# Three weight turns: two by VectorE blocks and transfers, one behind attention

## The chip, the cores and the metric

The kernel runs on one core of one Trainium2 chip. The metric is the device time of one execution in microseconds; lower is better. It is given as the median over several runs. One further execution was profiled, and the engine times below are from it.

## The reference

One image of 256 channels and 48 x 48 positions, that is 2304 tokens, goes through two layers, all in float32.

- Layer 0: group norm, then q, k and v projections (`xt @ Wq.T` and so on, so the weights are needed turned), an attention in which every head of every token is a row of one softmax over 9216 keys of width 64, the output projection `O @ Wo.T + bo`, and the residual.
- Layer 1, attention part: layer norm, `h = x @ W0 + b0`, slice weights `sw = softmax(h @ Ws + bs)`, an attention between 64 slice tokens, and `out @ Wout + bout`, with the residual.
- Layer 1, experts: layer norm, gate logits `xf @ Wg + bg`, the best two of 8 experts per token, a GELU network of width 1024 in each, and the residual.

The kernel folds small products of weights: `W0 @ Ws` gives the slice logits straight from the tokens, and `Wout @ Wg` (with `bout @ Wg`) gives the part of the gate logits that comes out of layer 1's attention. To multiply such a product on TensorE, W0 and Wout must stand turned in SBUF, as `W0T` and `WoutT`.

## The kernel before, in words

**Projections (0 to 66 us).** SyncE issues all loads in written order: x, Wq, Wk, Wv, Wo, some biases, W0, Ws, Wqkv, Wg, Wout in eight pieces, and two stores of zeros. `transposed` turns a 256 x 256 matrix by four TensorE transposes of 128 x 128 into one PSUM bank (`pw`), which ScalarE copies to SBUF. Wq, Wk and Wv are turned ahead of the projections, Wo after the first block of tokens, W0 and Wout after the first of the 18 tiles of v. `slice_weights` multiplies W0T and Ws into `Wl`, `centred` takes the mean out of `Wl`, and `gate_weights` multiplies WoutT and Wg into the last eight columns of `Wout_sb` and `bout_bc`. These stand in the loop over the v tiles, at `i == 3`, `6` and `9`. Nothing here is issued in a fixed order except what goes through `pe`, `dve`, `act` or `pool`: a scheduler places the plain `nc.` instructions. PSUM's eight banks are five for `pp` (q, k and v), one for `pgb` and two for `pw`.

**Attention of layer 0 (66 to 1216 us).** 18 blocks (`b`) of 512 query rows each run over 36 pairs of key tiles. `scores` makes two banks of `s` on TensorE, ScalarE takes the exponential into `p`, `times_values` multiplies it by v into two banks of `av`, and VectorE adds up `p` in `acc`. All of these engines' instructions stand in written order. Small steps of the finished blocks (`follow`, `between`) are strewn in between; their results use the banks `pa` and `pb` of pool `ps_side`. `out_proj` needs WoT, first for block pair g = 0. Its `move` brings VectorE's 32 x 32 blocks of `turned` to their places by 32 transfers per two token tiles, issued by SyncE (line 466). PSUM's banks are taken in the order of the pools: `ps_s` (0 to 3), `ps_av` (4, 5), `ps_side` (6, 7).

**Behind attention (1216 to 1260 us).** The last block is closed apart: `between(NQB - 1, ...)` sums `both` over the partitions into `pb` on TensorE and adds `busy(4, pa)`, four matmuls of 256 columns whose results nobody reads; `invert_few` turns `pb` on VectorE, inverts it and turns it back into `rinv`; `divide` makes `OT`. `out_proj` of the last group follows (`pm`), then `slices`, the turned slice weights (`pt`, `swT`), `busy(2, spin)`, and the sums `pts` and `den` once `sw` is there. Later `Wout_sb` with its gate columns is used once, for `tw`.

The last two steps in the block's closing, as written:

```python
half = close(behind, last=True)
invert_few, divide, extremes = between(NQB - 1, behind)
invert_few()
half(1, pool)
half(0, dve)
divide()
```

**Routing and experts (1260 us to the end).** Top-2 choice, slots, gathered rows, two matmul layers per slot, and the output.

## Time and profile before

| | us |
|---|---|
| Median of three runs | 1588.09 (1587.11 to 1591.71) |
| The profiled execution, its own time | 1585.05 |
| its span | 1583.3 |
| TensorE busy in it | 1561.7 |
| VectorE busy | 1037.0 |
| ScalarE busy | 829.6 |
| GpSimd busy | 257.6 |
| First scores of attention start at | 66.47 |
| Last matmul into `av` starts at | 1214.5 |

The names of a row are out<-in by the program's tiles, with buffer numbers left out. L61 is the line of the helper through which `pe`, `dve`, `act` and `pool` issue, so the tiles tell those rows apart. PE is TensorE, DVE VectorE, ACT ScalarE, POOL GpSimd, and SPq the queue on which SyncE issues transfers. A float32 matmul is recorded as two passes, so one turn of a matrix by four transposes is x4 and a product of two 256-column pieces is x4 as well. In a timeline a row is: start, time, engine, line, operation, tiles, shape, count, and in brackets the idle time just before it and what ended that.

### The profile page before, as it was taken

The page shows a single profiled execution, that of the slowest core. Times are in us where ns is not written, and L with a number is a line of the kernel's source. Part 1 is how long each engine was busy: PE and PEld are TensorE (multiplying, and loading weights), DVE is VectorE, ACT ScalarE, POOL GpSimd, SP SyncE. Part 2 cuts the span into 40 slices and gives each one's busy share as a digit, 9 for nine tenths or more (in the row PEclk, how much of TensorE's full clock was granted, in tenths as well). Part 3 has the DMA queues.
Part 4 walks back from the last instruction along what each step waited for, and adds up shares of the span by engine and source line. Part 5 has one row for each costly group of instructions (what it writes and reads, how often), then busy time and mean ns, then how long its engine had stood idle before and what let it go on. Part 6 is the DMA issues. An engine that isn't in the chain of part 4 may idle for free. (4 is left out here: it accounts for less than half of the span.)

```text
span 1583.3 us, 32283 instructions
## 1 busy us (share of the span) xinstructions
PE 1561.7 (99%) x13123; PEld 780.2 (49%) x13123; DVE 1037.0 (65%) x1324; ACT 829.6 (52%) x1168; POOL 257.6 (16%) x198
## 2 busy tenths in 40 slices
PE   9999999999999999999999999999999999999998
PEld 5633343333333333333333333333334789999996
DVE  7578787787777778878778778787787631211112
ACT  3356565565665656556556566566564533333331
POOL 0001001011010010110101101101010135766661
PEclk9999999999999999999999999999999999999999
DMA  4000000000000000000000000000000956666665
GB/s 137 1 1 1 1 1 3 6 1 1 9 1 1 8 1 2 7 2 2 4 5 2 2 8 1 1 8 1 1 2 21 335 168 177 186 180 190 194 172 160
DMA packets 52750, 79.32 MB, mean 50 GB/s; under 512 B 22527, under 2 KB 43214, under 8 KB 47470
## 3 DMA queue, kind: packets, MB, share of 16 engines
q1 hardware_dynamic: 42834, 66.45, 13.0%
q0 software_dynamic: 9104, 10.10, 3.8%
q8 instruction: 108, 1.77, 0.5%
q10 hardware_dynamic: 652, 0.56, 0.1%
q14 instruction: 52, 0.43, 0.1%
HBM read 62.94 MB, written 12.32 MB: 48 GB/s over the span
## 5 line engine op out<-in xcount | busy, mean ns | idle before, releaser
L61 ACT ACTIVATE p<-s 128x1024 f32<-128x1024 f32 x648 | 662.7, 1023 | 471.1 <-PE s L61 469.3
L61 DVE TENSOR_TENSOR acc<-acc,p 128x1024 f32<-128x1024 f32 x612 | 749.1, 1224 | 243.5 <-ACT p L61 237.6
L61 PE MATMUL av<-p,v_sb 64*64 64x512 f32 x5184 | 675.7, 590 | 3.2 <-ACT p L61 2.0
L61 PE MATMUL s<-q,kk 64*64 64x512 f32 x5184 | 674.8, 589 | 0.5 <-DVE tn L61 0.5
L61 PEld LDWEIGHTS s<-q,kk 64*64 64x64 f32 x5184 | 202.1, 133 | 353.6 <-issue 181.5
L61 PEld LDWEIGHTS av<-p,v_sb 64*64 64x64 f32 x5184 | 195.6, 131 | 358.7 <-ACT p L61 201.7
L61 POOL PARTITION_ALL_REDUCE total<-both x17 | 71.1, 4185 | 1011.8 <-ACT p L61 833.8
L61 ACT ACTIVATE hid<-ph,bcol 128x128 f32<-128x128 f32 x312 | 88.7, 369 | 197.6 <-PE ph L61 145.5
L61 PEld LDWEIGHTS ph<-xT,w 128*128 128x128 f32 x1248 | 145.2, 192 | 3.9 <-issue 1.7
L61 PE MATMUL ph<-xT,w 128*128 128x128 f32 x1248 | 145.9, 275 | 1.2 <-PEq L1398 0.7
L61 PE MATMUL py<-w_sb,hid 128*128 x624 | 144.0, 379 | 0.9 <-issue 0.7
L61 DVE TENSOR_TENSOR y<-py,b_bc 128x256 f32<-128x256 f32 x39 | 16.5, 424 | 176.1 <-PE py L61 136.9
L61 PEld LDWEIGHTS py<-w_sb,hid 128*128 128x128 f32 x624 | 114.6, 190 | 15.2 <-issue 1.3
L1244 POOL DMA_INDIRECT xs<-tn_d,part_t x88 | 90.0, 1022 | 29.9 <-issue 25.9
L1244 POOL DMA_INDIRECT t_d<-y,slot_t x38 | 61.3, 1613 | 77.4 <-DVE xT L61 32.7
L61 DVE COPY xT<-pt 128x256 f32<-128x256 f32 x17 | 7.0, 424 | 57.0 <-PE pt L61 57.0
L61 DVE RECIPROCAL rinv<-rinv 128x256 f32<-128x256 f32 x17 | 29.7, 1745 | 0.0
L61 POOL TENSOR_TENSOR rstd_t<-ve,mhalf 128x2 f32<-128x2 f32 (+2 forms) x13 | 11.1, 850 | 104.9 <-DVE ve L61 97.3
L61 DVE TENSOR_TENSOR acc<-p 128x1024 f32<-128x1024 f32 x18 | 22.1, 1225 | 4.9 <-ACT p L61 3.3
L340 DVE TENSOR_SCALAR q<-pp,bcol 64x512 f32<-64x512 f32 (+1 forms) x30 | 20.8, 694 | 5.9 <-PE pp L323 5.4
L61 DVE TENSOR_REDUCE up<-av 128x512 f32<-128x1024 f32 x17 | 20.8, 1224 | 5.0 <-PE av L61 5.0
L61 PE MATMUL spin<-Wqkv_sb,ident 128*128 128x256 f32 x82 | 19.2, 382 | 0.0
(306 smaller groups left out, 618.5 us busy)
## 6 DMA issues: line engine op xcount, KB each, us to landing
w<-in_L_ffn_W_dram SPq DMA_DIRECT2D x39, 1024.0 KB
w_sb<-in_L_ffn_W_dram SPq DMA_DIRECT2D x8, 1024.0 KB
t_sb<-turned SPq DMA_DIRECT2D x224, 8.0 KB
x_sb<-in_x_dram SPq DMA_DIRECT2D x3, 576.0 KB
t_d<-t_sb SPq DMA_DIRECT2D x2, 768.0 KB
tn_d<-tn SPq DMA_DIRECT2D x2, 768.0 KB
t_sb<-t_d SPq DMA_DIRECT2D x3, 512.0 KB
out_dram<-ob SPq DMA_DIRECT2D x3, 512.0 KB
```

What stands on the lines that cost most here:

```text
L61: return self.tc.keep_in_program_order(getattr(self.engine, name)(*args, **kwargs))
L340: nc.vector.tensor_scalar(dst, pq[rows, 0:tn], bcol[rows, B_Q + m : B_Q + m + 1], 0.125, ALU.add, ALU.mult,)
L1244: new = nc.gpsimd.indirect_dma_start(**kwargs)
```

## The change

- `turned_by_blocks` is new. VectorE turns the 32 x 32 blocks of a 256 x 256 matrix in one instruction of 128 x 512, and 32 transfers on SyncE's queue, each 32 rows of two runs of 128 bytes, bring the blocks to their places. Wo and W0 go this way, both called after the first block of tokens.
- `slice_weights` and `centred` stand at `i == 9` and `13` of the v loop instead of `3` and `6`.
- `gate_weights` is gone. Wout is turned by TensorE into `pa` after the last block of attention, where `busy(4, pa)` becomes four transposes and `busy(3, pb)`; ScalarE copies it into `turned`. The product with Wg takes the place of `busy(2, spin)`, in bank `spin`, and ScalarE copies it out.
- Attention's PSUM pools are opened in the order `ps_av`, `ps_side`, `ps_s`.
- `brep` has two parts instead of four.

```diff
+        def turned_by_blocks(dst, raw, name):
+
+            t = pj.tile([P, 2, C], FP, name=f"{name}_turned")
+            nc.vector.transpose(t.rearrange("p c n -> p (c n)"), raw.rearrange("p c n -> p (c n)"))
+            for a in range(4):
+                for k in range(4):
+                    for co in range(2):
+                        nc.sync.dma_start(
+                            out=dst[k * 32 : (k + 1) * 32, :, co * P + a * 32 : co * P + (a + 1) * 32],
+                            in_=t[a * 32 : (a + 1) * 32, co, :].rearrange("r (ci k s) -> r ci k s", ci=2, k=4)[
+                                :, :, k, :
+                            ],
+                        )
+            return dst
...
             if bi == 0:
                 later_constants()
-                transposed(WoT, raws["Wo"])
+                turned_by_blocks(WoT, raws["Wo"], "Wo")
+                W0T = turned_by_blocks(pj.tile([P, 2, C], FP, name="W0T"), W0_sb, "W0")
...
-            for k, b in enumerate((B_0, B_0 + 1, B_OUT, B_OUT + 1)):
+            for k, b in enumerate((B_0, B_0 + 1)):
...
-        def gate_weights():
...
-        brep = pj.tile([P, 4, P], FP, name="brep")
+        brep = pj.tile([P, 2, P], FP, name="brep")
...
-            if i == 0:
-                W0T = transposed(pj.tile([P, 2, C], FP, name="W0T"), W0_sb)
-                WoutT = transposed(pj.tile([P, 2, C], FP, name="WoutT"), Wout_sb)
-            elif i == 3:
+            if i == 9:
                 slice_weights()
-            elif i == 6:
+            elif i == 13:
                 centred()
-            elif i == 9:
-                gate_weights()
...
-        ) as at_p, tc.tile_pool(name="att1", bufs=1) as at_1, tc.tile_pool(name="ps_s", bufs=2, space=PSUM) as ps_s, tc.tile_pool(
+        ) as at_p, tc.tile_pool(name="att1", bufs=1) as at_1, tc.tile_pool(
             name="ps_av", bufs=1, space=PSUM
-        ) as ps_av, tc.tile_pool(name="ps_side", bufs=1, space=PSUM) as ps_side:
+        ) as ps_av, tc.tile_pool(name="ps_side", bufs=1, space=PSUM) as ps_side, tc.tile_pool(
+            name="ps_s", bufs=2, space=PSUM
+        ) as ps_s:
...
-                    busy(4, pa)
+                    for ci in range(2):
+                        for co in range(2):
+                            pe.transpose(
+                                pa[:, (2 * ci + co) * P : (2 * ci + co + 1) * P],
+                                Wout_sb[:, co, ci * P : (ci + 1) * P], ident,
+                            )
+                    busy(3, pb)
...
+                def keep_turned():
+                    act.copy(turned.rearrange("p c n -> p (c n)"), pa)
+
...
             invert_few()
+            keep_turned()
...
-    busy(2, spin)
+    gates = spin[:, 0 : 3 * E].rearrange("p (c e) -> p c e", c=3)
+    for ci in range(2):
+        for k in range(2):
+            pe.matmul(
+                gates[:, ci, :], turned[:, k, ci * P : (ci + 1) * P], Wl[:, k, S : S + E],
+                start=(k == 0), stop=(k == 1),
+            )
+    for k in range(2):
+        pe.matmul(
+            gates[:, 2, :], bcol[:, B_OUT + k : B_OUT + k + 1].to_broadcast([P, P]), Wl[:, k, S : S + E],
+            start=(k == 0), stop=(k == 1),
+        )
+    act.copy(Wout_sb[:, :, C : C + E], gates[:, 0:2, :])
+    act.copy(bout_bc[:, C : C + E], gates[:, 2, :])
```

More of the change, by code (lines that the diff above doesn't have):

```diff
@@ L379, in centred @@
             )
-        def gate_weights():
-            pw = ps_w.tile([P, 512], FP, name="pw", tag="pw")
-            for ci in range(2):
-                for k in range(2):
-                    nc.tensor.matmul(
-                        pw[:, ci * E : (ci + 1) * E], WoutT[:, k, ci * P : (ci + 1) * P],
-                        Wl[:, k, S : S + E], start=(k == 0), stop=(k == 1),
-                    )
-            for k in range(2):
-                nc.tensor.matmul(
-                    pw[:, 2 * E : 3 * E], brep[:, 2 + k, :], Wl[:, k, S : S + E],
-                    start=(k == 0), stop=(k == 1),
-                )
-            nc.vector.tensor_copy(
-                Wout_sb[:, :, C : C + E], pw[:, 0 : 2 * E].rearrange("p (c e) -> p c e", c=2)
-            )
-            nc.vector.tensor_copy(bout_bc[:, C : C + E], pw[:, 2 * E : 3 * E])
-        brep = pj.tile([P, 4, P], FP, name="brep")
+        brep = pj.tile([P, 2, P], FP, name="brep")
         for i in range(NTT):
@@ L734, in extremes @@
                     dve.tensor_reduce(ends_of[:, 1, b : b + 1], rinv, AX.X, ALU.max)
+                def keep_turned():
+                    act.copy(turned.rearrange("p c n -> p (c n)"), pa)
                 if b == NQB - 1:
-                    return invert_few, divide, extremes
+                    return invert_few, divide, extremes, keep_turned
                 work.extend([(12, sides), (13, invert), (14, divide), (15, extremes)])
@@ L772, in attention @@
             half = close(behind, last=True)
-            invert_few, divide, extremes = between(NQB - 1, behind)
+            invert_few, divide, extremes, keep_turned = between(NQB - 1, behind)
             invert_few()
+            keep_turned()
             half(1, pool)
```

## The prediction

> **What bounds the kernel now.** I read the page's busy table first, then its clock slices, then the timelines of the two stretches that the change touches.

> ```profile
> PE 1561.7 (99%) x13123; PEld 780.2 (49%) x13123; DVE 1037.0 (65%) x1324; ACT 829.6 (52%) x1168; POOL 257.6 (16%) x198
> ```

> TensorE is busy for 99% of the span, so a microsecond taken out of its stream, or put into it as a wait, is a microsecond of the end. The change touches only the projections (0 to 66 us) and the stretch behind attention (1215 to 1242 us). TensorE's timeline of the first:

> ```profile
> 47.11 0.60 PE L61 MATMUL pw<-ident,W_sb 128*128 128x128 f32 x4
> 47.55 0.60 PE L61 MATMUL pw<-ident,Wout_sb 128*128 128x128 f32 x4
> 47.98 2.75 PE L404 MATMUL pp<-WvT,t_sb 128*128 128x256 f32 x12
> 50.58 1.00 PE L358 MATMUL pw<-Ws_sb,W0T 128*128 128x64 f32 x8
> ...
> 57.54 0.95 PE L386 MATMUL pw<-Wl,WoutT 128*128 128x8 f32 x8
> 58.35 0.59 PE L391 MATMUL pw<-Wl,brep 128*128 128x8 f32 x4
> 58.80 7.15 PE L404 MATMUL pp<-WvT,t_sb 128*128 128x256 f32 x32
> 66.47 1.95 PE L61 MATMUL s<-q,kk 64*64 64x512 f32 x16 [0.52 <-DVE tn L61]
> ```

> There is no gap until 66.47, where the first scores wait 0.52 us for VectorE's last v eviction. To cost transfers that SyncE issues, its timeline: its last load, the first two lines of the existing transfers of this very shape (32x2x32, 64 runs of 128 bytes), and their row by source line.

> ```profile
> 21.53 0.70 SPq L224 DMA_DIRECT2D t_d<-empty  x1
> ...
> 269.66 11.91 SPq L466 DMA_DIRECT2D t_sb<-turned  x17
> ```
> ```profile
> 280.98 10.49 SPq L466 DMA_DIRECT2D t_sb<-turned  x16
> ```
> ```profile
> L466 SPq DMA_DIRECT2D t_sb<-turned x224: 585/595/1692, 269.7 to 1056.8; - x112
> ```

> One issue occupies SyncE for 595 ns. A burst of 32 takes 21.8 us (269.66 to 291.46), 0.68 us each. The seven bursts lie between 21.2 and 22.5 us.

> The stretch behind attention, TensorE and then VectorE:

> ```profile
> 1216.52 0.65 PE L61 MATMUL pb<-both,ones 128*64 128x256 f32 x4 [0.90 <-DVE both L61]
> 1217.10 1.99 PE L61 MATMUL pa<-Wqkv_sb,ident 128*128 128x256 f32 x8
> 1219.20 1.97 PE L61 MATMUL pm<-OT,WoT 128*128 128x256 f32 x8
> ```
> ```profile
> 1217.22 0.45 DVE L61 STREAM_TRANSPOSE rinv<-pb 128x256 f32<-128x256 f32 x1 [0.16 <-PE pb L61]
> ...
> 1219.04 0.42 DVE L61 TENSOR_TENSOR OT<-o,rinv 128x256 f32<-128x256 f32 x1
> ```

> VectorE starts on pb as soon as its sums are there, beside TensorE's filler. The chain pb, rinv, OT, pm paces this stretch.

> [...] the trace has the same pair in turned (0.44 us for 128x256) and L466. [...] the issues follow each other at 0.64 us, and the packets of a burst end 1.45 us after the last issue began, so issuing sets the pace. [...] in the view by windows (PEclk is third from the end):

> ```profile
> 1225.31:1228.72 3.41, 1.70 (x14) 1.51 (x14) 1.88 (x8) 1.59 (x7) 0.00 (x0) 1.00 0.95 320
> 1228.73:1232.14 3.41, 3.41 (x12) 3.10 (x13) 1.84 (x7) 0.42 (x1) 0.00 (x0) 0.50 1.10 361
> ```

> A window with TensorE half busy is followed by one at 0.50. At the start the first matmuls run at a pitch of 0.43 us and from 6.8 us at 0.22.

> **The change, part by part.** *Taken from TensorE ahead of attention:* Wo's four turns, 0.44 us (21.75 to 22.19); W0's and Wout's, 0.87 (47.11 to 47.98); Wout's product with Wg, 1.26 (57.54 to 58.80). Together 2.57 us, all on the path.

> *Added on SyncE:* 64 transfers, behind all loads. SyncE is free at 22.24. In the built program WoT's 32 stand before W0T's 32, and each waits for the transfer eight before it (five microseconds back at this pitch, so landed). With 0.68 us each, the last starts at 22.3 + 63 x 0.68 = 65.1 and lands about 1.45 later, at 66.6; with the pitches of the slowest and fastest burst (0.66 to 0.71), 65.3 to 68.5. Nothing else is queued behind them on SyncE until L466 at 269 us, and POOL gets nothing.

> *The wait this adds:* slice_weights needs W0T, and in TensorE's instruction order it now stands behind 14 of the 18 v tiles, its first matmul waiting for the last transfer but one, its third for the last. TensorE gets there at 46.25 - 0.44 + 14 x 0.865 = 57.9 us (0.865 is the pitch of a v tile, 7.15 - 0.22 us over 8). It stands until 66.6 - 0.64 = 66.0: **8.1 us idle.** Queued behind it are slice_weights (1.28), a v tile (0.86), centred (0.39), three v tiles (2.59), 5.1 us in all, then all of attention. The 2.57 us saved lie ahead of this wait and only lengthen it. For the cold clock I take 2.4 us: [...] none at all is the lower bound. The first scores still wait for the last v eviction in the program, although the new PSUM order gives them other banks than the last v tiles had, so the 0.52 stays (bound: 0 to 0.52). First score: 66.0 + 5.1 + 2.4 + 0.5 = 74.0 against 66.47, **+7.6 us** (+3.4 to +10.4).

> *Costed at nothing:* two block turns of 128x512 on VectorE, which no row shows; from 0.44 for half the size about 0.8 each, between the normalizations at 15 to 20 us. Their sources have landed by then (SyncE's next transfers on the same lanes went out at 14.84 and 17.25). q's evictions come some 0.6 us later, covered by five PSUM buffers; if that cover were gone, 1.6 us, absorbed by the 8 us wait. ScalarE loses three copies of 0.58, where it idles. ScalarE's first exponential and VectorE's tn wait for the same transfers, since their buffers take over the projections' space; they have landed by then. Attention's 36 blocks in other banks: same instructions, nothing either way (bound +-1 us).

> *Behind attention:* Wout's turns (0.44) and three fillers (3 x 0.45) replace four fillers (4 x 0.45): equal on TensorE. But the fillers now write pb, and VectorE's turn of pb waits, in the program, for the last of them instead of for the sums. It starts at 1217.10 + 0.44 + 1.34 + 0.2 = 1219.1 instead of 1217.22: **+1.9 us** on rinv, OT, pm and all after. TensorE then idles 2 us before OT, which may bring another half-clock window: +0.5 (0 to 1.7). The six 128x8 products (1.26) take the place of two fillers (0.89) in front of a 1.41 us idle wait for sw: hidden; without that cover 0.4. ScalarE's copies, 0.58 and two of about 0.2, fall into idle stretches (1217.8 to 1223.3, 1226.6 to 1228.4). W2's loads wait for pm's end and shift with everything. Sum: +2.4.

> Total +10.0 us. The profiled execution took 1585.05 (span 1583.3 and 1.75 around it) and would take 1595.1; the median of the runs, 1588.09, lies 3.0 above it, so the forecast is 1598.1.

> **The rivals.** *The transfers are in time (not slower).* SyncE's loads of 32 rows (Wout_sb) went out every 0.46 us. At that pace the last W0T lands at 22.3 + 63 x 0.46 + 1.45 = 52.7, ahead of 57.9; the front gains 2.6, the tail loses 1.9, and the time is 1587.4. It decides below 0.55 us per issue ((57.9 + 0.64 - 1.45 - 22.3) / 63). Against it: 224 issues of the same shape, none under 585 ns. *The wait without the cold clock:* front +5.2, tail +1.9: 1595.2. Against it stands the 0.50 window above, after far less idleness. *The tail's wait isn't there* (VectorE is released by the sums after all): front +7.6 alone, 1595.7; speaking for it is only that pb's halves are different columns. *The PSUM order does what it is arranged for,* scores without the eviction: 0.5 less of any of these.

> **How the numbers follow.** Forecast 0.60, no cold clock 0.14, no tail wait 0.12, transfers in time 0.10, others 0.04, counted as faster. The front's lower bound with no tail wait gives +3.4 (1591.5); its upper bound with the tail's 1.9 and 1.7 and the 1 us for attention's banks +15.0 (1603.1): that is the range, and it leaves out mainly the transfers in time. About 0.3% (4.8 us) is what a measurement of this kernel can tell from no change: slower beyond that 0.86, within 0.10, faster 0.04.

> **What would show it.** Right: 64 issues on SyncE from 22.3 to about 66 us; an idle gap of some 8 us on TensorE ahead of the matmuls from W0T into pw, released by a DMA; a stretch at 0.50 after it; first scores near 74; the first STREAM_TRANSPOSE of rinv about 2.5 us after pb's sums began instead of 0.7. Wrong: TensorE unbroken at 58 us, or an issue pitch under 0.55, or rinv's turn before the fillers' end.

## The result, and the profile after

The changed kernel takes 1599.15 us, the median of five runs (1595.78 to 1602.69), against 1588.09: the ratio is 1.007, with a 95% interval of 1.0058 to 1.0082. That is some 11 us slower. Its profiled execution took 1595.78 us with a span of 1594.0, which is 10.7 more than the span before.

The page of the changed kernel: the busy time of TensorE, and its granted clock in 40 slices of 40 us.

```profile
PE 1564.4 (98%) x13108; PEld 778.7 (49%) x13109; DVE 1038.0 (65%) x1322; ACT 830.0 (52%) x1168; POOL 257.9 (16%) x198
...
PEclk9899999999999999999999999999999999999999
```

Here 13108 recorded matmul passes are busy for 2.7 us longer than 13123 were before. Fewer passes and more time suggest that some of them ran slower. The second slice, 40 to 80 us, has a clock digit of 8: the place to look.

TensorE's timeline of that place, in the changed kernel (a float32 product counts as two passes, a transpose as one):

```profile
45.41 12.25 PE L401 MATMUL pp<-WvT,t_sb 128*128 128x256 f32 x56
65.17 1.97 PE L374 MATMUL pw<-Ws_sb,W0T 128*128 128x64 f32 x8 [7.51 <-DMA W0T<-W_turned]
66.93 1.06 PE L379 MATMUL pw<-Ws_sb,brep 128*128 128x64 f32 x4
67.78 2.02 PE L401 MATMUL pp<-WvT,t_sb 128*128 128x256 f32 x4
...
74.01 1.95 PE L61 MATMUL s<-q,kk 64*64 64x512 f32 x16 [0.52 <-DVE v_sb L405]
```

After 56 passes of v (14 tiles) TensorE stands idle for 7.51 us, and a DMA into `W0T` releases it. The eight passes that follow took 1.00 us before (at 50.58); here they take 1.97. The wait for the last v eviction, 0.52, is unchanged.

SyncE's queue in the same stretch, and its row by source line (issue time shortest/median/longest, then first and last issue):

```profile
22.43 21.29 SPq L271 DMA_DIRECT2D WoT<-Wo_turned  x32
43.82 20.78 SPq L271 DMA_DIRECT2D W0T<-W_turned  x32
```
```profile
L271 SPq DMA_DIRECT2D W0T<-W_turned x32: 585/595/597, 43.8 to 64.0; - x32
```

W0T's burst only begins when WoT's ends, and no issue is under 585 ns. The last issue but one, for which TensorE's first product waits, begins at 63.37; TensorE starts 1.8 us after it.

The view by windows shows the clock (start and end, length, busy time and count of PE, PEld, DVE, ACT and POOL, PEclk, DMA share, GB/s):

```profile
57.66:65.17 7.51, 0.00 (x1) 0.00 (x0) 0.42 (x1) 0.00 (x0) 0.00 (x0) 0.71 0.09 13
65.17:71.02 5.85, 5.85 (x22) 5.40 (x23) 1.15 (x4) 0.00 (x0) 0.00 (x0) 0.50 0.02 4
71.02:74.00 2.98, 2.47 (x12) 1.83 (x10) 1.31 (x4) 0.00 (x0) 0.00 (x0) 1.00 0.00 0
...
1231.54:1234.95 3.41, 2.46 (x24) 2.37 (x22) 2.28 (x11) 2.50 (x10) 0.70 (x1) 1.00 0.59 168
1234.96:1238.37 3.41, 3.03 (x13) 2.74 (x13) 0.76 (x4) 0.37 (x4) 0.00 (x0) 0.50 1.06 359
1238.38:1241.78 3.40, 3.35 (x12) 3.05 (x13) 1.84 (x7) 0.51 (x1) 0.00 (x0) 0.50 1.10 347
```

TensorE behind attention, and VectorE beside it:

```profile
1223.35 0.65 PE L61 MATMUL pb<-both,ones 128*64 128x256 f32 x4 [0.89 <-DVE both L61]
1223.93 0.66 PE L61 MATMUL pa<-ident,Wout_sb 128*128 128x128 f32 x4
1224.43 1.46 PE L61 MATMUL pb<-Wqkv_sb,ident 128*128 128x256 f32 x6
1226.52 0.67 PE L61 MATMUL pm<-OT,WoT 128*128 128x256 f32 x2 [0.63 <-DVE rinv L61]
1227.97 1.56 PE L61 MATMUL pm<-OT,WoT 128*128 128x256 f32 x6 [0.78 <-DVE OT L61]
...
1235.04 2.07 PE L61 MATMUL pts<-sw,tn 128*128 128x128 f32 x8 [1.03 <-DVE sw L61]
```
```profile
1225.92 0.45 DVE L61 STREAM_TRANSPOSE rinv<-pb 128x256 f32<-128x256 f32 x1 [2.03 <-PE pb L61]
...
1227.01 0.37 DVE L61 TENSOR_TENSOR o<-up,low 64x256 f32<-64x256 f32 x1
1227.49 0.42 DVE L61 TENSOR_TENSOR OT<-o,rinv 128x256 f32<-128x256 f32 x1
```

VectorE's turn of `pb` starts 2.57 us after the sums began, when the filler into `pb` has ended, instead of 0.70. TensorE then waits twice, for VectorE's turn of `pb` into `rinv` and for `OT`.

The difference of the two profiled executions, stage by stage ("first pts" is the first product of `sw` with `tn`):

| stage | before | after | difference |
|---|---|---|---|
| start to first scores | 66.47 | 74.01 | +7.54 |
| attention, to the sums in pb | 1150.05 | 1149.34 | -0.71 |
| sums in pb to OT | 2.52 | 4.14 | +1.62 |
| OT to first pts | 7.63 | 7.55 | -0.08 |
| first pts to tw | 14.38 | 15.71 | +1.33 |
| tw to the end | 342.28 | 343.25 | +0.97 |

The first line is the bulk, the third and fifth are the tail. Neither the second nor the last is tied to the change: over the kernels below the last stretch took anything from 339 to 346 us, and attention, where its first exponential was not late, 1149.3 to 1150.4.

### The profile page after: what moved, and what is told of

It is laid out like the page before. It is cut to its first block, busy times and chain, and to the rows that moved or that the text cites. A ratio compares the mean times of both kernels' runs of the same rounds, so it can differ in the third digit from the quotient of the medians.

```text
span 1594.0 us, 32286 instructions
## 1 busy us (share of the span) xinstructions
PE 1564.4 (98%) x13108; PEld 778.7 (49%) x13109; DVE 1038.0 (65%) x1322; ACT 830.0 (52%) x1168; POOL 257.9 (16%) x198
## 5 line engine op out<-in xcount | busy, mean ns | idle before, releaser
L61 ACT ACTIVATE p<-s 128x1024 f32<-128x1024 f32 x648 | 663.4, 1024 | 480.2 <-PE s L61 474.2
L61 DVE TENSOR_TENSOR acc<-acc,p 128x1024 f32<-128x1024 f32 x612 | 749.5, 1225 | 243.5 <-ACT p L61 237.4
L61 PE MATMUL av<-p,v_sb 64*64 64x512 f32 x5184 | 674.9, 590 | 2.3 <-ACT p L61 1.2
L61 PE MATMUL s<-q,kk 64*64 64x512 f32 x5184 | 673.8, 589 | 0.5 <-DVE v_sb L405 0.5
L61 PEld LDWEIGHTS s<-q,kk 64*64 64x64 f32 x5184 | 200.2, 133 | 355.5 <-issue 182.8
L61 PEld LDWEIGHTS av<-p,v_sb 64*64 64x64 f32 x5184 | 194.6, 131 | 359.0 <-ACT p L61 201.4
L61 POOL PARTITION_ALL_REDUCE total<-both x17 | 71.2, 4186 | 1019.7 <-ACT p L61 833.7
L61 ACT ACTIVATE hid<-ph,bcol 128x128 f32<-128x128 f32 x312 | 89.3, 369 | 199.4 <-PE ph L61 120.9
L61 PE MATMUL ph<-xT,w 128*128 128x128 f32 x1248 | 146.2, 275 | 1.9 <-issue 1.0
L61 PEld LDWEIGHTS ph<-xT,w 128*128 128x128 f32 x1248 | 145.3, 192 | 4.7 <-issue 2.5
L61 PE MATMUL py<-w_sb,hid 128*128 x624 | 144.5, 380 | 1.5 <-issue 1.1
L61 DVE TENSOR_TENSOR y<-py,b_bc 128x256 f32<-128x256 f32 x39 | 16.6, 425 | 179.1 <-PE py L61 121.8
L61 PEld LDWEIGHTS py<-w_sb,hid 128*128 128x128 f32 x624 | 114.4, 190 | 16.4 <-issue 2.5
L61 DVE COPY xT<-pt 128x256 f32<-128x256 f32 x17 | 7.0, 424 | 56.3 <-PE pt L61 56.3
L61 DVE RECIPROCAL rinv<-rinv 128x256 f32<-128x256 f32 x17 | 29.7, 1746 | 0.0
L61 POOL TENSOR_TENSOR rstd_t<-ve,mhalf 128x2 f32<-128x2 f32 (+2 forms) x13 | 11.1, 852 | 107.0 <-DVE ve L61 100.3
L61 DVE TENSOR_TENSOR acc<-p 128x1024 f32<-128x1024 f32 x18 | 22.1, 1226 | 4.8 <-ACT p L61 3.2
L61 DVE TENSOR_REDUCE up<-av 128x512 f32<-128x1024 f32 x17 | 20.8, 1225 | 5.0 <-PE av L61 5.0
L61 PE MATMUL spin<-Wqkv_sb,ident 128*128 128x256 f32 x78 | 18.2, 382 | 0.0
```

The lines of the kernel that those rows point to most:

```text
L61: return self.tc.keep_in_program_order(getattr(self.engine, name)(*args, **kwargs))
```

## The experiments

Each ratio is against the kernel before on the same chip. The chips differ (the kernel before had 1580.81, 1583.37, 1580.3 and 1583.19 us on the four used), so ratios are compared, not times; one thousandth is 1.6 us. Even ratios differ by about that much between chips: one kernel that ran on two of them gave 0.9988 and 0.9998. A diff is against the changed kernel unless another is named.

**W0T's transfers first.**

```diff
-                turned_by_blocks(WoT, raws["Wo"], "Wo")
                 W0T = turned_by_blocks(pj.tile([P, 2, C], FP, name="W0T"), W0_sb, "W0")
+                turned_by_blocks(WoT, raws["Wo"], "Wo")
```

> The changed kernel with the two calls swapped, so that W0T's 32 transfers stand ahead of WoT's on SyncE; the same 64 transfers. Theory (TensorE waits for the last of 64 issues at 0.64 to 0.68 us each): W0T lands near 44.5 us, TensorE runs through the projections without a gap, first scores near 63.2 us instead of 74.0; the last transfer still lands near 65.5, and ScalarE's first exponential, whose buffer lies over the source of the transfers, waits for it some 1.2 us longer than for its scores. In all about 9.5 us less than the changed kernel: near 1589.5. Rival (the loss comes from somewhere else in the front, PSUM's order or VectorE's block turns): no gain over the changed kernel, 1599.

Measured: 1584.01 us, ratio 1.0025 (1.0018 to 1.0032). TensorE had no gap and the first scores began at 63.64, close to the 63.2 expected and 10.37 us sooner than in the changed kernel. But not all of that arrived. The timeline of all engines in this kernel:

```profile
63.64 1.95 PE L61 MATMUL s<-q,kk 64*64 64x512 f32 x16 [0.52 <-DVE v_sb L405]
...
66.92 0.06 DVE L61 MEMSET tn<- 128x4 f32 x1 [3.34 <-DMA WoT<-Wo_turned]
67.08 1.94 ACT L61 ACTIVATE p<-s 128x1024 f32<-128x1024 f32 x2 [20.13 <-DVE tn L61]
68.15 1.09 PE L61 MATMUL av<-p,v_sb 64*64 64x512 f32 x8 [2.57 <-ACT p L61]
```

The first exponential comes 3.44 us after its scores began; after the W0T wait, in the changed kernel, it was 1.28 (74.01 to 75.29). VectorE's `tn` waits for the last WoT transfer, and ScalarE behind `tn`: a wait of 2.2 us has taken the place of the longer one. The order of two calls was worth 0.0045, some 7 us, of the whole loss. The closing code behind attention is the changed kernel's, with the same delays of `rinv` and OT, yet this execution has no half-clock window there.

**The fillers into the other bank, ahead of the transposes.**

```diff
+                    busy(3, pa)
                     for ci in range(2):
...
-                    busy(3, pb)
```

> The changed kernel with the three fillers behind attention written to pa ahead of Wout's turns, instead of to pb after them; nothing else. Theory (VectorE's turn of pb waits for the last filler): the turn starts 0.7 us after the sums' start instead of 2.6, OT comes 1.6 to 1.9 us sooner, and with one half-clock window less up to 1.3 more: 1.6 to 3 us less than the changed kernel, near 1596.8; the 8 us gap in the front stays. Rival (only the front costs anything): 1599, and OT no sooner.

Measured: 1592.29 us, ratio 1.0066 (1.0052 to 1.008). In the trace `rinv` started 0.70 us after the sums and OT 2.52, as before the change. But OT to first pts became 8.23 us instead of 7.55, so that 0.68 of the 1.62 us was lost again, and the time can't be told from the changed kernel's. The mechanism was right and most of the gain was not there.

**Both.** The two diffs above together.

> The edits of the two runs before together. Theory: the gains add, about 12 us less than the changed kernel: near 1587, 0 to 2 us under the kernel before. Rival (the two waits are not independent or a third cost remains): over 1590.

Measured: 1583.53 us, ratio 1.0019 (1.0012 to 1.0026), so still slower. The first exponential waited as with W0T's transfers first (3.51 us after its scores began). TensorE behind attention shows what ate the other gain:

```profile
1215.28 0.65 PE L61 MATMUL pb<-both,ones 128*64 128x256 f32 x4 [0.90 <-DVE both L61]
1215.86 1.56 PE L61 MATMUL pa<-Wqkv_sb,ident 128*128 128x256 f32 x6
1217.26 0.60 PE L61 MATMUL pa<-ident,Wout_sb 128*128 128x128 f32 x4
1218.54 1.99 PE L61 MATMUL pm<-OT,WoT 128*128 128x256 f32 x8 [0.68 <-ACT turned L61]
```

With the fillers ahead, Wout's transposes end at 1217.9; ScalarE's copy of `pa` starts only then, and `pm` waits 0.68 us for it. VectorE's OT had started at 1217.80, as early after the sums as before the change (2.52 us). So where the fillers stand decides which reader of these two banks is late, VectorE at `pb` or ScalarE at `pa`. The profiled execution of this kernel was 1.5 us under its own median, and that of W0T first 1.7; what the other runs lost more is not shown.

**W0 by TensorE again, Wo by blocks.**

```diff
-                W0T = turned_by_blocks(pj.tile([P, 2, C], FP, name="W0T"), W0_sb, "W0")
...
-            if i == 9:
+            if i == 0:
+                W0T = transposed(pj.tile([P, 2, C], FP, name="W0T"), W0_sb)
+            elif i == 9:
```

> The changed kernel with W0 alone turned by TensorE again, after the first v tile; Wo keeps its block turn and 32 transfers, so SyncE is done near 44 us. Theory (the wait for W0T is the front's loss): no gap on TensorE, first scores near 63.7 us (57.7 + 0.44 + 5.1 + 0.5) and the first exponential waits for nothing else, 10.3 us less than the changed kernel: near 1588.9. Rival (Wo's transfers or the later place of slice_weights cost too): first scores later than 65 us.

Measured: 1581.16 us, ratio 1.0002 (0.9993 to 1.001): the loss is gone. TensorE, then ScalarE, in this kernel:

```profile
54.58 1.00 PE L373 MATMUL pw<-Ws_sb,W0T 128*128 128x64 f32 x8
...
63.95 1.95 PE L61 MATMUL s<-q,kk 64*64 64x512 f32 x16 [0.52 <-DVE v_sb L404]
65.23 1.94 ACT L61 ACTIVATE p<-s 128x1024 f32<-128x1024 f32 x2 [17.64 <-PE s L61]
```

The eight passes from W0T take 1.00 us again, and with no second burst on SyncE the first exponential follows its scores in 1.28. The front is 2.5 us better than before; the tail's wait (rinv 2.58 after the sums) and a second half-clock window are still in and take that back. This shows that W0T's transfers and the wait for them are the whole loss of the front.

**The same, with the fillers in a bank that has been read out.** Against the kernel just above:

```diff
-                    busy(3, pb)
+                    busy(3, st["av"][:, 0, :])
```

> The changed kernel with W0 turned by TensorE, and with the three fillers behind attention written over the av bank, which is read out by then, instead of to pb. In the run where they went to pa ahead of Wout's turns, VectorE started at once but out_proj waited for ScalarE's copy of the late turns; here the turns stay first and nothing waits for the fillers. Theory (the front's wait and the fillers' wait are all that the change costs): first scores near 64 us, rinv 0.7 us after the sums' start, OT 2.5 us after it, then 7.6 us to the first product of sw with tn: 2 to 3 us under the kernel before, a ratio near 0.9985. Rival (a further cost in the new places of the gate products or in PSUM's order): ratio 1.000 or more.

Measured: 1580.84 us, ratio 0.9988 (0.9978 to 0.9997), close to what was expected; a second measurement below gave 0.9998. `rinv` started 0.69 us after the sums, OT 2.52, and OT to first pts took 7.54: neither of the two waits.

**TensorE kept busy through the wait.** 36 products of 96 columns into `pgb`, right ahead of `slice_weights`; its matmuls are issued through `pe` so that they stay behind them, and the two steps stand at `i == 13` and `14`, which gives the changed kernel's order.

```diff
+            for _ in range(36):
+                pe.matmul(pgb, ones, ones[:, 0:96], start=True, stop=True)
```

> The changed kernel with 36 matmuls of 96 columns that nobody reads put on TensorE just ahead of slice_weights, behind the 14th v tile, so that it is busy while it waits for W0T. Theory (the wait costs 8 us as such and 2.4 to 3 us more by the half clock after it): clock 1.00 throughout the front, slice_weights to first scores 5.7 us instead of 8.8, so 3 us less than the changed kernel, still about 8 over the kernel before (ratio 1.005). Rival (the clock record is without effect on the time): the stretch stays at 8.8 us and the ratio at 1.007.

Measured: 1597.18 us, ratio 1.0085 (1.0061 to 1.0109). TensorE's timeline and a window of it:

```profile
57.48 8.17 PE L61 MATMUL pgb<-ones 128*128 128x96 f32 x72
65.96 1.32 PE L61 MATMUL pw<-Ws_sb,W0T 128*128 128x64 f32 x8 [0.31 <-DMA W0T<-W_turned]
...
72.20 1.95 PE L61 MATMUL s<-q,kk 64*64 64x512 f32 x16 [0.52 <-DVE v_sb L407]
```
```profile
65.90:72.20 6.30, 5.69 (x33) 4.82 (x33) 2.45 (x8) 0.00 (x0) 0.00 (x0) 1.00 0.01 1
```

The clock stayed at 1.00, and from the first matmul of W0T to the first scores it took 6.24 us instead of 8.84: at least 2.6 us of the front were the cold (half) clock. W0T landed 0.8 us later, so 1.8 are left in the front. The time doesn't show them: the profiled execution has a gap of 3.33 us in the experts at 1326 us, which nothing in the edit touches, and the interval holds everything from a small gain to a loss. The trace is clear, the time isn't.

**The filler's bank alone, in the kernel before.** Against the kernel before:

```diff
-                    busy(4, pa)
+                    busy(4, pb)
```

> The kernel before with one word changed: the four fillers behind attention go to pb instead of pa. Theory (the fillers' bank alone makes VectorE wait): rinv starts 2.5 us after the sums' start instead of 0.7, OT 1.6 us later, and the kernel is 1.6 to 2.9 us slower than before (ratio 1.001 to 1.0018). Rival (Wout's turns or the copy cause the later start in the changed kernel): no difference.

Measured: 1584.96 us, ratio 1.0007 (0.9999 to 1.0015). VectorE in this kernel, where the sums into `pb` began at 1215.66:

```profile
1218.28 0.45 DVE L61 STREAM_TRANSPOSE rinv<-pb 128x256 f32<-128x256 f32 x1 [2.07 <-PE pb L61]
...
1219.37 0.38 DVE L61 TENSOR_TENSOR o<-up,low 64x256 f32<-64x256 f32 x1
1219.85 0.43 DVE L61 TENSOR_TENSOR OT<-o,rinv 128x256 f32<-128x256 f32 x1
```

The turn starts 2.62 us after the sums and OT 4.19 after: +1.92 and +1.67, as in the changed kernel (2.57 and 4.14). The same four products, in other columns of the bank that VectorE is to read, make the wait. In time that is +1.1 us (-0.2 to +2.4); this execution happened to have no half-clock window behind attention.

**The old order of the PSUM pools,** on the kernel with W0 by TensorE and the fillers over `av`: `ps_s`, `ps_av`, `ps_side`.

> The run with W0 by TensorE and the fillers over av, with attention's PSUM pools back in their old order. Theory (the first scores wait for the last v eviction in either order): first scores at the same time, again after a wait of about 0.5 us, and no difference in time (within 1 us). Rival (the new order frees the first scores' banks earlier): 0.5 us or more later here.

Measured: 1581.58 us, ratio 0.9992 (0.9984 to 0.9999), against 0.9988 with the new order on the same chip. First scores at 63.83 and 63.81, both after the same 0.52 us. The order of the pools does nothing that shows.

**Everything by blocks, with both waits removed.** W0T's transfers first, the fillers over `av`, and the source tile in the pool that outlives the projections, so that no tile of attention takes the space that the transfers still read:

```diff
-            t = pj.tile([P, 2, C], FP, name=f"{name}_turned")
+            t = l0.tile([P, 2, C], FP, name=f"{name}_turned")
```

> Both matrices by blocks and transfers, W0T's transfers first, the fillers over av, and the two turned source tiles kept in the layer's pool instead of the projections' pool, so that the first exponential's buffer no longer lies over the source of WoT's transfers. Theory (in the runs with W0T first, what was left of the loss is ScalarE's first exponential waiting for the last of the 64 transfers, 2.2 us in the profile and more in other executions): first scores near 63.3 us, the first exponential 1.3 us after them instead of 3.4 to 3.5, first product with v near 65.7; 2.5 to 3.5 us under the kernel before (ratio 0.998). Rival (64 transfers beside the start of attention cost something else): first exponential on time, but ratio 1.000 or more.

Measured: 1579.61 us, ratio 0.9996 (0.9987 to 1.0004). The timeline of this kernel:

```profile
63.54 1.95 PE L61 MATMUL s<-q,kk 64*64 64x512 f32 x16 [0.52 <-DVE v_sb L405]
64.82 1.94 ACT L61 ACTIVATE p<-s 128x1024 f32<-128x1024 f32 x2 [17.97 <-DMA WoT<-Wo_turned]
```

The exponential comes 1.28 us after its scores again, though SyncE issues WoT's transfers until 65.56 (the profile names one of them as the last release in ScalarE's long idle stretch; the start is nevertheless the usual one, with the first scores done). What had waited was the reuse of their source's space. With that and the moved fillers the ratio is 0.0023 (3.6 us) better than with both edits alone, though on another chip; the trace shows 2.2 us of it at the exponential and 0.68 at `pm`. Still, it is less than the 0.998 expected, only level with the kernel before.

**W0 by TensorE and fillers over av, a second time,** beside the last one on the same chip.

> The kernel with W0 by TensorE and the fillers over av once more, to stand beside the other on one chip. Theory: its first scores come 0.4 us later than the other's for W0's turn on TensorE, otherwise the same; a ratio of 0.9985, the two within 1 us of each other. Rival (transfers cost as such): this one is faster by 1 us or more.

Measured: 1579.27 us, ratio 0.9998 (0.9989 to 1.0006). So the way by transfers, with all its waits removed, and TensorE's own turn of W0 are equal, though TensorE has four transposes less to do in one of them. In both, TensorE waits 1.03 us for `sw` with the gate products ahead of it, and both had half-clock windows behind that (one each in these profiles).

**The two fillers kept ahead of the gate products,** on each of these two kernels:

```diff
+    busy(2, spin)
     gates = spin[:, 0 : 3 * E].rearrange("p (c e) -> p c e", c=3)
```

> The run with both matrices by blocks, W0T first, the fillers over av and the sources in the layer's pool, with busy(2, spin) kept, ahead of the six gate products instead of being replaced by them. Open is where the 2.7 us that its trace gains ahead of attention go: the time showed 0.7 us (ratio 0.9996). Theory [...]: one window or none at 0.50 behind attention, the idle time before the product of sw with tn shrinks from 1.0 to about 0.15 us, and 1 to 1.5 us less time: ratio near 0.9987. Rival (the windows are chance): ratio 0.9996 as before.

> The same two fillers kept in the kernel with W0 by TensorE and the fillers over av, which stood at ratios of 0.9988 and 0.9998. Theory: near 0.9985, one half-clock window or none. Rival: 0.9993, the mean of the two.

Measured: by transfers 1580.15 us, ratio **0.9979** (0.9971 to 0.9988), 3.0 us under the 1583.19 of the kernel before; with W0 by TensorE 1581.06, ratio **0.9985** (0.9979 to 0.9992). Both are faster than the kernel before, by the intervals on this chip; between the two the intervals overlap. TensorE's timeline of the second:

```profile
1221.50 1.03 PE L61 MATMUL spin<-Wqkv_sb,ident 128*128 128x256 f32 x4
1222.37 0.95 PE L61 MATMUL spin<-Wl,turned 128*128 128x8 f32 x8
1223.18 0.59 PE L61 MATMUL spin<-Wl,bcol 128*128 128x8 f32 x4
1223.94 1.16 PE L61 MATMUL pts<-sw,tn 128*128 128x128 f32 x8 [0.17 <-DVE sw L61]
```

The fillers fill the wait for `sw` (0.17 us left of 1.03), and `sw` comes no later. Against the same kernels without the fillers the ratios are 0.0017 (2.7 us) and 0.0008 (about 1.3 us, against the mean of two runs) better. But those ran on other chips, and differences of this size between chips were seen above, so a gain from keeping the fillers is not shown. Nor is it settled that there are fewer half-clock windows: first pts to tw took 12.95 us with none, 14.1 to 14.4 with one and 15.7 with two. The second kernel had none (mean granted clock 1.00 over 28 us from the sums in `pb`) where it had had one in each of two profiles (0.94 in both); the first had one as before (0.94 both times). And the count also varies where the code behind attention is the same: two in the changed kernel and none with W0T's transfers first, two for W0 by TensorE with fillers over `av` and the old PSUM order and one with the new (mean granted clock of the whole execution 0.997 and 0.998).

## Why the prediction was right

**The wait.** It said 64 issues at 0.68 us, TensorE reaching W0T at 57.9 and resuming at 66.0. Measured: 57.66 and 65.17, a gap of 7.51 instead of 8.1. The 64 issues came every 0.66 us, so the last began at 64.0 instead of 65.1. A part of that was lost again: the 1.45 us after an issue is when its packets end, but TensorE was let go only 1.8 us after it. The term that carried the wait, the issue time of 0.595 us read off the existing transfers of the same shape, held to the nanosecond; the rival of transfers in time fell with it. W0 by TensorE, and W0T's transfers first, show the cause.

**The cold clock.** The 2.4 us, and the upper bound of the front with it, rested on how long half clock would last after such a gap. That was its author's estimate; no trace of the kernel before shows it. Measured: full clock to 60.78 us, 3.12 after the last matmul ended, then half clock to 71.02. The cost was about 2.9 us, not 2.4. At full clock the stretch from W0T to the first scores takes about 5.9 us, and it took 8.84. The 5.9 is 9.38 us in the kernel with W0T's transfers first, less four v tiles of 0.86 that stand in it there. The prediction had put 5.6 for this work, so its sum was short by 0.5 for the clock and 0.3 for the work. Resuming 0.8 early and running 0.8 slower cancelled: 74.0 was hit (74.01) by opposite misses, which is luck. Keeping TensorE busy removed 2.6 us; the other 0.3 went into W0T's eight passes, which took 1.32 us there instead of 1.00, since the last transfer, issued at 64.79, was still under way. The rival without the cold clock fell on that trace.

```profile
54.26 1.00 PE L374 MATMUL pw<-Ws_sb,W0T 128*128 128x64 f32 x8
...
63.64 0.66 PE L61 MATMUL s<-q,kk 64*64 64x512 f32 x4 [0.52 <-DVE v_sb L405]
```

**The tail.** `rinv` was to start 1.9 us later; it did by 1.87. The prediction carried that to OT in full, but OT came only 1.62 later: VectorE's `o` took 0.37 instead of 0.63 us. Before, GpSimd's `o` (0.72 us from 1217.93) ran beside it, from 1218.31; in the changed kernel GpSimd's had ended at 1225.49, ahead of VectorE's at 1227.01. The bank alone in the kernel before gave the same delay, so the rival without a tail wait is out. The half-clock windows were put at +0.5 (0 to 1.7) and came to 1.33 in the profiled execution; the same closing code had none in the kernel with W0T's transfers first, so this term deserves its range more than its value.

**Costed at nothing.** VectorE's block turns were estimated at 0.8 us each: each took 0.71, and after 15 us TensorE had no wait until W0T's.

```profile
14.59 0.71 DVE L267 STREAM_TRANSPOSE Wo_turned<-Wo_raw 128x512 f32<-128x512 f32 x1
```

ScalarE's first exponential was said to wait for the same transfers, which would have landed; so it was, but only because TensorE's longer wait hid it. With W0T's transfers first it was 2.2 us. The gate products were hidden, as said; that fillers went for them was not thought of, and what that cost at the clock is not shown. Attention came 0.71 shorter, within the +-1 allowed, but other banks are not shown as the reason: with the old order on W0 by TensorE it took 1149.33 us, with the new 1149.96. The PSUM order did nothing for the first scores, as costed. One slip in the text: attention has 18 blocks of 36 pairs, not 36 blocks; no number hangs on it.

**The sum.** 7.54 in the front, 1.62 and 1.33 in the tail against 7.6, 1.9 and 0.5: with the stages costed at nothing (-0.71, -0.08, +0.97) that makes the 10.7 of the spans, against 10.0. The median was forecast at 1598.1 and came to 1599.15: it lies 3.4 us above the profiled execution, where 3.0 had been taken over from the kernel before. The 1.33 and the 0.97 could as well have been smaller in another execution.

## What to carry to other kernels

Before work goes from a busy engine to small transfers, multiply their number by the issue time of one on the queue that issues them (64 at 0.66 us here), and put the end of that sum beside the moment when the operand is needed; order the transfers by who needs them first. Once they are late, look also at who takes over the space of their source. And a filler that nobody reads has a bank, and a place in front of a wait: both count when it is moved or replaced.

## What was not expected of the hardware

Standing still for 7.51 us cost about 10.4 up to the first scores, as much as W0T's transfers first brought back (10.37): 2.9 us more were lost at half clock, since full speed came back only 5.85 us after the restart.

Behind attention TensorE's busy time did not tell which stretch was followed by half clock. Two stretches of the changed kernel:

```profile
1224.73:1228.14 3.41, 2.00 (x9) 1.14 (x8) 2.04 (x6) 0.48 (x1) 0.72 (x1) 1.00 0.00 0
```
```profile
1231.54:1234.95 3.41, 2.46 (x24) 2.37 (x22) 2.28 (x11) 2.50 (x10) 0.70 (x1) 1.00 0.59 168
```

TensorE was busy for 2.00 us of the first and for 2.46 us of the second. The first was followed by full clock (1.00 from 1228.15 to 1231.53), the second, though busier, by half clock (0.50 from 1234.96 to 1241.78). What sets them apart is not shown, and so it stays open why the number of half-clock windows behind attention varies.

And writing one half of a PSUM bank held up the reading of the other half until the last write: with the fillers alone put there in the kernel before, VectorE's turn of `pb` started 2.62 us after the sums instead of 0.70, 1.9 later. The wait stands in the program, so whether the hardware would need it wasn't tried.
